# Three groups' transposes and copies ahead of their distance products, and the context norms added on VectorE, in a one-core gated cross-attention kernel

## The chip, the cores and the metric

The kernel runs on one core of a Trainium2 chip. The metric is the device time of one execution in microseconds (us), lower is better. Engines: TensorE multiplies matrices into PSUM, ScalarE (ACT in the profile) evaluates activations, VectorE (DVE) does elementwise work, GpSimd (POOL) does some of both, and SyncE (SP) issues most transfers. Each engine runs its own instructions in order; semaphores join them.

## What is computed

Inputs are `x` and a context, 32 samples of 128 rows by 128 features. Four parts follow each other, each added to `x`: gated attention of `x` on the context, a quantized feed-forward layer, an alignment of each sample's rows with its context rows, and eight experts behind a global threshold. The change touches the seam between the second and the third:

```python
# second part, its last product
acc = jnp.einsum('bsh,oh->bso', xq - zx, wq)
return acc * (sx * sw) + b
...
# third part: a = context of one sample, b = layernorm(x) of that sample
def _pairwise_euclidean(a, b):
    aa = jnp.sum(a * a, axis=-1)[:, None]
    bb = jnp.sum(b * b, axis=-1)[None, :]
    ab = a @ b.T
    return jnp.sqrt(jnp.maximum(aa + bb - 2.0 * ab, 0.0))
...
D = _pairwise_euclidean(small, large)
R = _dtw_cost(D)          # R[i,j] = D[i,j] + min of three neighbours
```

The table R is walked back to an alignment, which picks the context rows that are added to `x`.

## The kernel before

**Tiles.** Samples go in groups of 4 (`GB`)[...]. The alignment is split in two parts: the first 12 samples (`NP = 3` groups) and the other 20. The first part's distances are made in the stage that the change touches. The second part's are made by ScalarE, TensorE and GpSimd (`second_dense`, L1226) while VectorE runs the first part's alignment.

**The stage.** `dense_steps` (L950) loops over the three groups. For each, `dense` (L903) quantizes the hidden layer (VectorE L906, ScalarE L909, VectorE L910), multiplies it by the second weight (TensorE L916) and adds to `X` (VectorE L921). `norm_steps` (L193), fed in between, makes the layer norm of groups 0 and 1 together and then of group 2: statistics (L155 on), a root by Newton steps (L182 to L190), the normalized rows `y` (VectorE L211) and their transposes into the PSUM tile `tp` (TensorE L215). Then it calls `take`, which calls `distances` (L924) for the group:

- ScalarE copies `tp` twice: `ym2` is minus two times it (L926), `ysq` its square (L928).
- TensorE sums in `d2`: `ones` times `ysq` (L931) puts the square norms of `y` in every row, and four products of the context `CD` with `ym2` (L933) add the cross terms.
- ScalarE adds the context norms `aa`, one number per row and sample, and clips at zero (`dd`, L939, once for each of four samples).
- ScalarE takes roots, rows 0 to 63 forward (L941) and rows 64 to 127 with the columns reversed (L942), into `dist`. The last of these is kept as `held["root"]`.
- Two transfers a group put the halves of `dist` into the DRAM tensor `d_dram` (L945), on SP's queue, except that the last group's second half goes on ScalarE's.

The pool `dist` holds two buffers of each of `hqt`, `ym2`, `ysq`, `dd` and `dist`; `distps` holds two PSUM banks each of `tp` and `d2`.

**Behind it.** `warp_steps` (L969) loads chunks of `d_dram` into `dc` (L1056, on SP) and runs the alignment rows on VectorE: two instructions a row, a minimum (L1072) and a scan (L1073), 64 rows. Then tables and a walk back (`hit`, L1101). `second_dense` starts on ScalarE behind `held["root"]` (L1162). The expert stage begins with `aligned(0)` (L1301) and holds 64 units of matmuls (L1470, L1483), between which VectorE's background steps (`pump`, L1408) do the second part's alignment and the threshold search (L1352).

**Order.** The code order isn't the order on the engines. A planner takes the whole program with its dependences and arranges each engine's instructions by the costs that it assumes; `tc.issue_after` adds an edge. Before, TensorE runs the transposes of groups 0 and 1, products 0 and 1, the transposes of group 2, product 2.

Of the kernel before, what the change touches and what calls it, by code (L numbers as in the profile page):

```python
# [8 lines left out]
F32 = mybir.dt.float32  # L9
# [3 lines left out]
AF = mybir.ActivationFunctionType  # L13
ALU = mybir.AluOpType
# [4 lines left out]
P = 128  # L19
B = 32  # L20
S = 128
# [7 lines left out]
GB = 4  # L29
# [4 lines left out]
SH = S // 2  # L34
# [3 lines left out]
NP = 3  # L38
# [5 lines left out]
def tile_flamingo_gated(  # L44
# [21 lines left out]
    nc = tc.nc  # L66

    def pool(stack, name, bufs=1, space=None, side=None):
        kw = {} if space is None else {"space": space}
        kw.update({} if side is None else {"side": side})  # L70
        return stack.enter_context(tc.tile_pool(name=name, bufs=bufs, **kw))

    def new(p, shape, dt, tag, bufs=None):
        kw = {} if bufs is None else {"bufs": bufs}
        return p.tile(shape, dt, tag=tag, name=tag, **kw)
# [7 lines left out]
    CD = new(keep, [P, B, S], F32, "CD")  # L83
# [45 lines left out]
    ones = new(keep, [P, P], F32, "ones")  # L129
# [18 lines left out]
    held = {}  # L148
# [44 lines left out]
    def norm_steps(p, psp, s0, n, take, tag, shape=None):  # L193

        xq = X[:, s0 : s0 + n, :]
        m, w = (8, "") if n <= 8 else (16, "_w")
        mean = new(p, [P, m], F32, "bn_mean" + w)[:, 0:n]
        r = new(p, [P, m], F32, "bn_r" + w)[:, 0:n]
        for _ in row_norm_steps(p, xq, n, mean, r):
            yield  # L200
        for h in range(n // GB):
            if shape is None:
                tp = new(psp, [P, GB, S], F32, tag)
            else:
                if h % 2 == 0:
                    pair = new(psp, shape, F32, tag)
                tp = pair[:, h % 2]
            for i in range(GB):
                j = GB * h + i
                y = new(p, [P, D], F32, "y", bufs=6)  # L210
                got = nc.vector.tensor_scalar(  # L211
                    y, xq[:, j, :], mean[:, j : j + 1], r[:, j : j + 1], ALU.subtract, ALU.mult
                )
                held["y"] = getattr(got, "ins", got)
                nc.tensor.transpose(tp[:, i, :], y, ident)  # L215
                if i % 2 == 1:
                    yield
            take(s0 // GB + h, tp)
            yield
# [70 lines left out]
    with ExitStack() as st:  # L290
# [47 lines left out]
        for k in range(2):  # L338
            nc.gpsimd.affine_select(
                out=mtmp[:, k], in_=mtmp[:, k], compare_op=ALU.is_ge, fill=0.0, base=-64 * k,  # L340
# [3 lines left out]
                out=mtmp[:, k], in_=mtmp[:, k], compare_op=ALU.is_ge, fill=0.0,  # L344
# [7 lines left out]
        for k in range(2):  # L352
            nc.gpsimd.affine_select(
                out=mneg[:, k], in_=mneg[:, k], compare_op=ALU.is_ge, fill=-BIG, base=SH - SH * k,
# [44 lines left out]
        for k in range(6):  # L399
# [3 lines left out]
                rhs=one_c[0:1, :], start=True, stop=True,  # L403
# [6 lines left out]
        for k in range(2):  # L410
            hr_ps = new(p_at, [P, 4, S], F32, "at")
            nc.tensor.matmul(
                hr_ps, lhsT=sel.rearrange("p j c h -> p (j c h)"),
                rhs=ind[:, 4 * k : 4 * k + 4, :], start=True, stop=True,
# [89 lines left out]
        def take(g, tp):  # L504
            nc.scalar.copy(YT[:, GB * g : GB * g + GB, :], tp)
            v = YT[:, GB * g : GB * g + GB, :].rearrange("p b s -> p (b s)")
            nc.vector.tensor_reduce(xst[:, 0, g : g + 1], v, AX.X, ALU.max)
            nc.vector.tensor_reduce(xst[:, 1, g : g + 1], v, AX.X, ALU.min, negate=True)
# [137 lines left out]
        def finish(s0, n, HN, d2, ms):  # L646
# [30 lines left out]
            for _ in norm_steps(lp, p_at, s0, n, take, "at"):  # L677
                yield
# [39 lines left out]
        for p in range(B // 2 + 1):  # L718
# [4 lines left out]
            for u in range(3):  # L723
# [6 lines left out]
                g = p // 2 + 1  # L730
# [47 lines left out]
    for n_s in (BP, B - BP):  # L778
        m = new(rest, [2 * n_s, 3], F32, f"mask{len(masks)}")
        for v, fill, low_side in ((0, -1.0, True), (1, -2.0 * S - 2.0, True), (2, 1.0, False)):  # L780
            nc.gpsimd.memset(m[:, v : v + 1], fill)
            nc.gpsimd.affine_select(
                out=m[:, v : v + 1], in_=m[:, v : v + 1], compare_op=ALU.is_ge, fill=0.0,
# [7 lines left out]
    d_dram = new(dram, [2, B, SH, S], F32, "d_dram")  # L791
# [6 lines left out]
    with ExitStack() as st:  # L798
# [18 lines left out]
        with ExitStack() as st2:  # L817
# [16 lines left out]
            def rounded(n):  # L834
                for k in range(2):
                    blk = YT[:, 8 * n + 4 * k : 8 * n + 4 * k + 4, :].rearrange("p b s -> p (b s)")
                    nc.scalar.activation(blk, blk, AF.Identity, bias=magic_c, scale=inv)
                    xq = XQ[:, 1024 * n + 512 * k : 1024 * n + 512 * k + 512]
                    nc.scalar.activation(xq, blk, AF.Relu, bias=low_x[:, 1:2])
                    got = nc.vector.tensor_scalar(xq, xq, 255.0, low_x[:, 0:1], ALU.min, ALU.add)  # L840
                return getattr(got, "ins", got)

            rounded(0)
            for n in range(4):
                for c in range(NC):
                    ph = new(p_h, [P, 2, 512], F32, "ph")
                    for k in range(2):
# [3 lines left out]
                            start=True, stop=True,  # L851
# [8 lines left out]
                    if c == 0 and n < 3:  # L860
                        got = rounded(n + 1)
# [15 lines left out]
        aa = new(rest, [P, B], F32, "aa")  # L877
# [43 lines left out]
        nc.vector.scalar_tensor_tensor(xb, po, s2, xb, ALU.mult, ALU.add)  # L921
        yield 0.7

    def distances(g, tp, dp, d2_new, queues):  # L924
        ym2 = new(dp, [P, GB, S], F32, "ym2")
        nc.scalar.activation(ym2, tp, AF.Copy, scale=-2.0)  # L926
        ysq = new(dp, [P, GB, S], F32, "ysq")
        nc.scalar.activation(ysq, tp, AF.Square)  # L928
        d2 = d2_new()
        dd = new(dp, [P, GB, S], F32, "dd")  # L930
        nc.tensor.matmul(d2, lhsT=ones, rhs=ysq, start=True, stop=False)  # L931
        for i in range(GB):
            nc.tensor.matmul(  # L933
                d2[:, i, :], lhsT=CD[:, GB * g + i, :], rhs=ym2[:, i, :],
                start=False, stop=(i == GB - 1),
            )
        for i in range(GB):
            b = GB * g + i
            nc.scalar.activation(dd[:, i, :], d2[:, i, :], AF.Relu, bias=aa[:, b : b + 1])  # L939
        dist = new(dp, [P, GB, S], F32, "dist")  # L940
        nc.scalar.activation(dist[0:SH], dd[0:SH], AF.Sqrt)  # L941
        got = nc.scalar.activation(dist[SH:P], dd[SH:P, :, ::-1], AF.Sqrt)  # L942
        held["root"] = getattr(got, "ins", got)
        for h in range(2):
            queues[h].dma_start(  # L945
                out=d_dram[h, GB * g : GB * g + GB].rearrange("b r j -> r b j"),
                in_=dist[SH * h : SH * h + SH],
            )

    def dense_steps(tie, dp, lp, po_new, psp, tag, take):  # L950
        ties = [tie, tie]
        behind = iter(())
        for n in range(NP):
            for _ in dense(n, ties[n], dp, po_new, ties):
                for _ in range(3):
                    next(behind, 0)
            if n % 2 == 1 or n == NP - 1:
                for _ in behind:
                    pass
                m = n % 2 + 1  # L960
                behind = norm_steps(lp, psp, GB * (n - m + 1), m * GB, take, tag)
        for _ in behind:
            pass
# [166 lines left out]
    with ExitStack() as st:  # L1130
        dp = pool(st, "dist", bufs=2)
        lp = pool(st, "lnA", bufs=2)
        p_o = pool(st, "p_o", bufs=2, space=PSUM)
        dps = pool(st, "distps", bufs=2, space=PSUM)

        def take(g, tp):
            distances(
                g, tp, dp, lambda: new(dps, [P, GB, S], F32, "d2"),
                (nc.sync, nc.scalar if g == NP - 1 else nc.sync),
            )  # L1140

        dense_steps(
            held["quantized"], dp, lp, lambda: new(p_o, [P, GB, D], F32, "po"), dps, "tp", take
        )
    parts[0].close()

    with ExitStack() as st:
        wp = pool(st, "warp", bufs=2, side="right")  # L1150
        w1p = pool(st, "warp1", side="right")
        dp = pool(st, "distB", side="right")
# [3 lines left out]
        dps = pool(st, "distpsB", space=PSUM)  # L1156
# [128 lines left out]
    with ExitStack() as st:  # L1285
# [176 lines left out]
        for n, (k, p, g, j) in enumerate(units):  # L1462
# [5 lines left out]
            for c in range(NC):  # L1468
                ph = new(p_h, [P, GB * S], F32, "mph")
                got = nc.tensor.matmul(  # L1470
                    ph, lhsT=w1e[:, j, c * P : (c + 1) * P], rhs=tok, start=True, stop=True
                )
                held["mm"] = getattr(got, "ins", got)
                hT.append(new(hp, [P, GB * S], F32, "hT"))
                got = nc.scalar.activation(  # L1475
                    hT[c], ph, AF.Gelu_apprx_tanh, bias=mb1s[:, e, c : c + 1]
                )
# [3 lines left out]
            for i in range(GB):  # L1481
                for c in range(NC):
                    got = nc.tensor.matmul(  # L1483
                        po[:, i, :], lhsT=hT[c][:, i * S : (i + 1) * S], rhs=w2e[:, j, c, :],
                        start=(c == 0), stop=(c == NC - 1),
                    )
# [55 lines left out]
```

## Time and profile before

| what | value |
|---|---|
| time, median of 3 runs | 868.48 us (868.47 to 871.42) |
| profiled execution | 869.44 us, span 867.7 us |
| TensorE busy | 692.2 us (80%), mean granted clock 0.861 |
| VectorE busy | 588.4 us (68%) |
| ScalarE busy | 453.2 us (52%) |
| `ym2`, L926, 128x512 from PSUM | 3 times, mean 605 ns |
| `ysq`, L928, 128x512 from PSUM | 3 times, mean 598 ns |
| `dd`, L939, 128x128 from PSUM | 12 times, mean 368 ns; four in a row 1.14 us |
| `dist`, L941 and L942, 64x512 | 3 times each, mean 629 and 626 ns |
| table load before the first root | once, 1283 ns |
| `d_dram<-dist`, L945 | 6 transfers, 128 KB each |

Granted clock in the windows of the stage, from the profile: 0.50 from 242 to 246 us, 0.60 from 246 to 248, 1.00 from 248 to 254, 0.60 from 254 to 256, 0.50 from 256 to 268.

How to read it: the profile shows one execution, on the time axis of its span. A product of 128x512 in f32 appears as two instructions, one of 128x128 also as two, so "L933 x8" is one group's four products. The chain of waits is followed back from the last instruction to what released it, and lists its pieces in order of time: start, length, engine, tile and line. In a timeline a row ends with the idle time before it in brackets and with what released it.

### The profile page before, as it was taken

To read this page: it belongs to the slowest core of one execution; us is meant where nothing else is said; L and a number is where in the kernel's file an instruction comes from. 1 tells how busy PE (TensorE), PEld (TensorE's weight loads), DVE (VectorE), ACT (ScalarE), POOL (GpSimd) and SP (SyncE) were. 2 spreads that over 40 slices of the span, in tenths; PEclk is the share of its full clock that TensorE was granted. 3 is DMA by queue.
4 is the path that set the end of the run, shared out by engine and by line. 5 is a ranking of instruction groups with operands and counts; after the bars stand their busy time and mean duration, and the time that the engine had idled before them with its cause. 6 is when DMAs were issued, how large, how long until landed. Compare 5 with 4: busy or idle time off the path is not lost.

```text
span 867.7 us, 13245 instructions
## 1 busy us (share of the span) xinstructions
PE 692.2 (80%) x4689; PEld 462.3 (53%) x4695; DVE 588.4 (68%) x2040; ACT 453.2 (52%) x803; POOL 66.8 (8%) x132
## 2 busy tenths in 40 slices
PE   5798998344251334478999999999999999999997
PEld 2244554211231222246777776876677777777775
DVE  7847998979835998879995376656614544444444
ACT  2778777496248978433444444434444333334442
POOL 2000000001301121100100101010000000000000
PEclk9898999555565555559999999999999999999999
DMA  8100000200012131012452111020013212121110
GB/s 322 37 2 12 2 3 2 81 18 0 0 25 52 29 73 44 13 35 80 145 158 89 62 62 61 25 74 37 37 39 96 62 37 85 37 61 49 50 61 25
DMA packets 20201, 47.32 MB, mean 55 GB/s; under 512 B 4014, under 2 KB 6942, under 8 KB 20110
## 3 DMA queue, kind: packets, MB, share of 16 engines
q1 hardware_dynamic: 14372, 29.69, 11.1%
q0 software_dynamic: 5056, 16.62, 6.1%
q8 instruction: 37, 0.61, 0.3%
q10 hardware_dynamic: 706, 0.16, 0.1%
q14 instruction: 30, 0.25, 0.1%
HBM read 27.12 MB, written 13.37 MB: 47 GB/s over the span
## 4 chain that ended last, share of the span: by engine, by line
PE 54%; DVE 20%; ACT 2%; issue 2%; DMA 1%; POOL 0%; SPq 0%; DVEq 0%; ACTq 0%
PE mph L1470 25%; PE mpo L1483 24%; DVE ru L1073 4%; DVE ru L1072 3%; DVE hit L1101 3%; DVE hst L858 2%; DVE hst L859 2%; PE px L1313 1%; PE small L1333 1%; DVE junk L1347 1%; PE po L916 1%; PE px L1327 1%; PE d L931 0%; DVE bn L155 0%; DVE lf L993 0%
## 5 line engine op out<-in xcount | busy, mean ns | idle before, releaser
L1483 PEld LDWEIGHTS mpo<-mw,hT 128*128 128x128 f32 x2048 | 249.6, 192 | 58.9 <-issue 39.4
L1475 ACT ACTIVATE hT<-mph,mb1s 128x512 f32<-128x512 f32 x256 | 175.7, 687 | 182.0 <-PE mph L1470 168.4
L1483 PE MATMUL mpo<-mw,hT 128*128 128x128 f32 x2048 | 256.1, 276 | 0.1
L1470 PE MATMUL mph<-YT,mw 128*128 128x512 f32 x512 | 245.3, 600 | 0.0
L1470 PEld LDWEIGHTS mph<-YT,mw 128*128 128x128 f32 x512 | 87.4, 193 | 57.9 <-issue 57.8
L1433 DVE TENSOR_TENSOR biased<-mpo,mb2s 128x512 f32<-128x512 f32 x28 | 19.4, 691 | 119.6 <-PE mpo L1483 119.6
L1438 DVE SCALAR_TENSOR_TENSOR X<-biased,GA,X 128x128 f32<-128x128 f32 x248 | 67.8, 345 | 0.1
L1491 ACT COPY ye<-mpo 128x512 f32<-128x512 f32 x34 | 19.9, 585 | 86.2 <-PE mpo L1483 83.6
L1073 DVE TENSOR_TENSOR_SCAN ru<-ru,dc 24x128 f32<-24x128 f32 (+1 forms) x128 | 54.0, 422 | 6.8 <-DMA dc<-d_dram 3.3
L1072 DVE TENSOR_TENSOR ru<-ru 24x128 f32<-24x128 f32 (+1 forms) x128 | 38.8, 303 | 3.1
L1492 POOL DMA_DIRECT2D y_dram<-ye x34 | 18.5, 543 | 228.4 <-ACT ye L1491 228.0
L562 ACT ACTIVATE dm<-bi 128x512 f32<-128x512 f32 x48 | 29.0, 606 | 8.0 <-PE bi L557 3.2
L604 DVE TENSOR_TENSOR sm<-sc,dm 128x512 f32<-128x512 f32 x32 | 21.7, 684 | 13.9 <-ACT dm L562 9.8
L1194 PE MATMUL po<-w2q,HT 128*128 128x128 bf16 x80 | 9.4, 313 | 24.6 <-ACT HT L1167 24.6
L849 PE MATMUL ph<-XQ,w1q 128*128 128x512 bf16 x31 | 15.6, 615 | 16.8 <-DVE XQ L840 9.5
L1261 PE MATMUL tp<-ident,y 128*128 128x128 f32 x20 | 8.1, 475 | 23.9 <-ACT y L1167 23.9
L1203 PE MATMUL d<-b,ones 128*128 128x512 f32 x10 | 10.0, 1107 | 18.0 <-ACT b L1167 18.0
L1101 DVE SCALAR_TENSOR_TENSOR hit<-jotab,vw,YT 24x128 bf16<-24x128 bf16 x59 | 21.1, 357 | 4.1 <-DMA YT<-dv 2.0
L518 ACT ACTIVATE qm<-YT,mcol 128x512 f32<-128x512 f32 x32 | 23.2, 732 | 0.0
L1433 DVE TENSOR_TENSOR biased<-yl,mb2s 128x512 f32<-128x512 f32 x34 | 23.1, 681 | 0.0
L538 PE MATMUL sc<-qm,CD 64*128 64x256 f32 x128 | 21.7, 449 | 0.6 <-ACT YT L379 0.6
L1194 PEld LDWEIGHTS <-HT 128*128 128x128 bf16 x80 | 8.1, 147 | 26.1 <-ACT HT L1167 26.1
(380 smaller groups left out, 1019.5 us busy)
## 6 DMA issues: line engine op xcount, KB each, us to landing
y_dram<-ye POOLq DMA_DIRECT2D x34, 256.0 KB, 2.3
yl<-y_dram SPq DMA_DIRECT2D x34, 256.0 KB
mw<-in_mw POOLq DMA_DIRECT2D x12, 512.0 KB, 4.5
rblk<-ru SPq DMA_DIRECT2D x10, 288.8 KB
X<-in_x SPq DMA_DIRECT2D x4, 512.0 KB
CD<-in_ctx_d SPq DMA_DIRECT2D x4, 512.0 KB
CT<-in_ctx_t SPq DMA_DIRECT2D x4, 512.0 KB
mw<-in_mw SPq DMA_DIRECT2D x4, 512.0 KB
```

What stands on the lines that cost most here:

```text
L518: nc.scalar.activation(held["qm", g][:, h], YT[:, GB * g : GB * g + GB, :], AF.Copy, scale=mcol[:, h : h + 1],)
L538: nc.tensor.matmul(scs[:, k, 4 * v : 4 * v + 4], lhsT=CD[kr, n, :], rhs=qm[kr, :, n % GB, SH:S], start=True, stop=True,)
L562: done = nc.scalar.activation(dm, bi, AF.Exp)
L604: got = nc.vector.tensor_tensor(sm, scs[:, u], dm, ALU.mult)
L1072: nc.vector.tensor_tensor(u, ru[:, r, 0, 1 : S + 1], ru[:, r, 0, 0:S], ALU.min)
L1073: got = nc.vector.tensor_tensor_scan(ru[:, r + 1, 0, 1 : S + 1], u, dc[:, r, :], BIG, ALU.min, ALU.add)
L1101: nc.vector.scalar_tensor_tensor(hit, jotab[0:H2], vw[:, r + 1 : r + 2], near[:, r - r0, :] if r >= r0 else DV[:, r, :], ALU.is_le, ALU.mu ...
L1433: nc.vector.tensor_tensor(t, y, bias, ALU.add)
L1438: nc.vector.scalar_tensor_tensor(X[:, b, :], v[:, i, :], GA[:, E * b + e : E * b + e + 1], X[:, b, :], ALU.mult, ALU.add,)
L1470: got = nc.tensor.matmul(ph, lhsT=w1e[:, j, c * P : (c + 1) * P], rhs=tok, start=True, stop=True)
L1475: got = nc.scalar.activation(hT[c], ph, AF.Gelu_apprx_tanh, bias=mb1s[:, e, c : c + 1])
L1483: got = nc.tensor.matmul(po[:, i, :], lhsT=hT[c][:, i * S : (i + 1) * S], rhs=w2e[:, j, c, :], start=(c == 0), stop=(c == NC - 1),)
```

## The change

`distances` goes. `take` now makes only the two copies `ym2` and `ysq` of a group, each in three buffers instead of two, and keeps them in a list. After `dense_steps` has written out all three groups, a loop over the list makes the products, the sum with the context norms, the roots and the transfers. The sum with `aa` and the clip at zero are one VectorE instruction for each sample in place of one ScalarE instruction. The roots, the buffers of `dd` and `dist`, the queues of the transfers and `held["root"]` stay as they were.

```diff
-    def distances(g, tp, dp, d2_new, queues):
-        ym2 = new(dp, [P, GB, S], F32, "ym2")
-        nc.scalar.activation(ym2, tp, AF.Copy, scale=-2.0)
-        ysq = new(dp, [P, GB, S], F32, "ysq")
-        nc.scalar.activation(ysq, tp, AF.Square)
-        d2 = d2_new()
-        dd = new(dp, [P, GB, S], F32, "dd")
...
-        for i in range(GB):
-            b = GB * g + i
-            nc.scalar.activation(dd[:, i, :], d2[:, i, :], AF.Relu, bias=aa[:, b : b + 1])
...
+        normed = []
+
         def take(g, tp):
-            distances(
-                g, tp, dp, lambda: new(dps, [P, GB, S], F32, "d2"),
-                (nc.sync, nc.scalar if g == NP - 1 else nc.sync),
-            )
+            ym2 = new(dp, [P, GB, S], F32, "ym2", bufs=NP)
+            nc.scalar.activation(ym2, tp, AF.Copy, scale=-2.0)
+            ysq = new(dp, [P, GB, S], F32, "ysq", bufs=NP)
+            nc.scalar.activation(ysq, tp, AF.Square)
+            normed.append((g, ym2, ysq))
...
+        for g, ym2, ysq in normed:
+            d2 = new(dps, [P, GB, S], F32, "d2")
+            nc.tensor.matmul(d2, lhsT=ones, rhs=ysq, start=True, stop=False)
+            for i in range(GB):
+                nc.tensor.matmul(
+                    d2[:, i, :], lhsT=CD[:, GB * g + i, :], rhs=ym2[:, i, :],
+                    start=False, stop=(i == GB - 1),
+                )
+            dd = new(dp, [P, GB, S], F32, "dd")
+            for i in range(GB):
+                b = GB * g + i
+                nc.vector.tensor_scalar(
+                    dd[:, i, :], d2[:, i, :], aa[:, b : b + 1], 0.0, ALU.add, ALU.max
+                )
+            dist = new(dp, [P, GB, S], F32, "dist")
+            nc.scalar.activation(dist[0:SH], dd[0:SH], AF.Sqrt)
+            got = nc.scalar.activation(dist[SH:P], dd[SH:P, :, ::-1], AF.Sqrt)
+            held["root"] = getattr(got, "ins", got)
+            for h in range(2):
+                (nc.sync, nc.scalar if g == NP - 1 else nc.sync)[h].dma_start(
+                    out=d_dram[h, GB * g : GB * g + GB].rearrange("b r j -> r b j"),
+                    in_=dist[SH * h : SH * h + SH],
+                )
```

More of the change, by code (lines that the diff above doesn't have):

```diff
@@ L922, in dense @@
         yield 0.7
-    def distances(g, tp, dp, d2_new, queues):
-        ym2 = new(dp, [P, GB, S], F32, "ym2")
-        nc.scalar.activation(ym2, tp, AF.Copy, scale=-2.0)
-        ysq = new(dp, [P, GB, S], F32, "ysq")
-        nc.scalar.activation(ysq, tp, AF.Square)
-        d2 = d2_new()
-        dd = new(dp, [P, GB, S], F32, "dd")
-        nc.tensor.matmul(d2, lhsT=ones, rhs=ysq, start=True, stop=False)
-        for i in range(GB):
-            nc.tensor.matmul(
-                d2[:, i, :], lhsT=CD[:, GB * g + i, :], rhs=ym2[:, i, :],
-                start=False, stop=(i == GB - 1),
-            )
-        for i in range(GB):
-            b = GB * g + i
[L939 to L948, printed above, removed]
     def dense_steps(tie, dp, lp, po_new, psp, tag, take):
@@ L1134, in tile_flamingo_gated @@
         dps = pool(st, "distps", bufs=2, space=PSUM)
+        normed = []
         def take(g, tp):
-            distances(
-                g, tp, dp, lambda: new(dps, [P, GB, S], F32, "d2"),
-                (nc.sync, nc.scalar if g == NP - 1 else nc.sync),
-            )
+            ym2 = new(dp, [P, GB, S], F32, "ym2", bufs=NP)
[3 more added lines that the diff above has]
+            normed.append((g, ym2, ysq))
         dense_steps(
```

## The prediction

> **What bounds the kernel now.** I read the page's slices first: TensorE is at 9 tenths from slice 18 on (the expert stage, a fixed amount of matmul), and before that its clock stands at 5 with gaps in its row, so there something else decides. Then the chain of waits over 222 to 275 us of the profiled execution, where the edited stage lies. It runs through that stage without a break and out of it over a DMA into the alignment rows on VectorE:
>
> ```profile
> 244.13 0.60 ACT ym L926
> 244.73 0.50 ACT ysq L928
> ...
> 245.27 2.07 PE d L931 x2
> 247.34 1.08 PE d L933 x8
> ...
> 248.45 1.14 ACT dd L939 x4
> ...
> 249.61 1.28 ACT L941
> 250.90 0.63 ACT dist L941
> ...
> 252.21 1.14 ACT dd L939 x4
> 253.35 0.49 ACT ym L926
> 253.83 0.49 ACT dist L941
> ...
> 254.35 0.63 ACT dist L942
> ...
> 255.00 0.60 ACT ysq L928
> ...
> 255.65 2.08 PE d L931 x2
> 257.72 1.72 PE d L933 x8
> ...
> 261.29 2.44 DMA d_dram<-dist
> ```
>
> The second column is how long each piece holds the chain. ScalarE serves three groups in a row; the copies of the third (ym at 253.35, ysq at 255.00) come behind the roots of the first two, so the third product starts only at 255.65. From the last root's end (261.29 + 0.63 = 261.92) to the first scan (268.10) it is 6.18 us of DMA out, issue, and DMA in. TensorE's own timeline shows what the late copies cost it:
>
> ```profile
> 248.25 1.02 PE L931 MATMUL d<-ysq,ones 128*128 128x512 f32 x2
> 249.11 1.05 PE L933 MATMUL d<-ym,CD 128*128 128x128 f32 x8
> 250.00 0.60 PE L215 MATMUL tp<-ident,y 128*128 128x128 f32 x4
> 255.65 2.08 PE L931 MATMUL d<-ysq,ones 128*128 128x512 f32 x2 [5.05 <-ACT ysq L928]
> ```
>
> The second product takes 1.9 us (248.25 to 250.16) at granted clock 1.00; the third, after 5.05 us of idling, 3.8 us (255.65 to 259.44) at 0.50. Everything after the first scan hangs on it: rows and hits on VectorE to 367, the first expert matmul at 381.7, then TensorE busy for 476 of the 484 us from 384 to 868 (24.6, 111.2, 107.1 and 233.1 in four windows). ScalarE's second stage starts at 261.94 from the same root. So I carry a shift of the last root one for one to the end.
>
> **The change, step by step**, on the clock of the profiled execution.
>
> *Transposes and copies.* Up to 245.27 nothing differs: the transposes of groups 0 and 1 and their copies already run ahead of product 0. The third group's y tiles leave VectorE at 247.21 (246.09 + 1.12). The planner seems to give an idle engine the ready instruction that stands first in the code (before, ym2 slipped in front of dist 1, whose operand was just not ready), so I let it start product 0 at 245.27 and put the third transposes next, now ahead of product 1: product 0 ends at 248.42, transposes at 249.02 (0.60), copies at 249.07 + 0.60 + 0.50 = 250.17. No root stands before them any more.
>
> *Products.* Product 1 from 249.02 ends at 251.0, product 2 follows at once, 1.9 us warm: 252.95. That is 6.5 us before today's 259.44, 1.9 of it from the clock.
>
> *Norms on VectorE.* Twelve ScalarE instructions go (three times 1.14 us) and twelve VectorE ones come. No row shows a two-operation tensor_scalar from PSUM at 128x128 f32. The nearest are y L211, same operation from SBUF, 341 ns, and X<-mpo L1438, same size from PSUM, 344 ns, 0.273 apart where 248 of its SBUF form follow each other. By them four cost 3 x 0.273 + 0.344 = 1.16 us. The Trainium skill speaks against the move ("VectorE: DVE Perf Modes", section on why PSUM operands drop a tier): f32 from PSUM loses the double rate that a scalar operation has from SBUF. At 0.96 GHz that is 67 ns on 128 elements, 408 each, 1.4 us for four; below 1.1 nothing speaks. I take 1.16, as the L1438 row reads PSUM. dd of group 0 ends 249.61, of group 2 at 254.15 (254.4 by the rule). VectorE has nothing else here: its next instruction before was at 264.63. What queues behind a dd on it are only those four memsets of the alignment.
>
> *Roots.* The table load (1.28) waited for its activation's operand elsewhere (at 383.82, right after the first expert product), so it starts behind both the copies and dd 0: 250.2 to 251.5. Roots 0 end at 252.78, roots 1 at 254.1 (0.63 each plus 0.03).
>
> *The new wait.* dist has two buffers, and group 2 writes the one of group 0, whose two transfers are issued at 252.1 and 252.8. One took 2.44 us to land, the ScalarE-issued one some 2.65 (the alignment's first memset, freed by it, ran at 264.63). Before, group 2 came 8 us later and never met this. Now buffer 0 is free at about 255.3, 1.2 us after dd 2 and roots 1. Bounds: nothing (6.4 us gained in all), or a wait for the first half alone (root end 256.0), or both halves; the copy b in the second stage waits 2.4 us for d_dram<-b with both halves out, so I take both: roots 2 run 255.35 to 256.64. Behind this wait on ScalarE stands only its second stage, tied to the last root anyway. It also covers the norms: dd 2 could be 1 us later for nothing.
>
> *DMAs.* The same six. The five on SP take 0.58 to 0.70 us to issue and their sources come every 0.66, so SP keeps step. ScalarE's one stays last. The first two moved 262 KB inside 251.6 to about 255; pairs may overlap a little more, 0 to 0.5 us. Two more copies of ym2 and ysq are 4 KB per partition and no time.
>
> *Sum*: 261.92 - 256.64 = 5.3 us. The profiled execution took 869.44 (span 867.7 and 1.74 around it), 0.96 over the median of the runs; the difference is taken from the median: **868.48 - 5.3 = 863.2**.
>
> **The clock as a rule.** The row shows the clock rising near 247.3, 4.5 us after the first transpose. The skill ("TensorE: Matmul & The Clock Gate", Part 1) says the window of some 3.4 us runs freely and the start of full speed varies from run to run. By the row the gain is 5.3; by the rule's latest phase (two windows, 249.6) product 0 and the third transposes stay cold: copies end 251.4, roots 0 at 254.0, buffer free at 256.5, last root 257.9, gain 4.0. Two of three runs agree to 0.01 us, so I take the row.
>
> **Rivals.**
>
> *The plan leaves the third transposes behind product 1* (the change doesn't do all it says). For: they stood there before. Against: in the code they now come first. They end at 250.6, dd 0 is ready at 249.6, so table load and a root pass before ym2; ysq2 ends at about 252.7, product 2 at 254.9 warm or 256.5 cold, dd 2 at 256.0 to 257.7, last root 257.4 to 259.0: gain 2.9 to 4.5, **864.8**.
>
> *Cold clock*, as above: **864.5**.
>
> *The gain is taken back later*, a transfer or ScalarE's second stage ending last: **868**. Against: last copies at 361.6 wait on a TensorE queue held by the alignment (9.06 us before a<-d), so ScalarE has slack.
>
> *Slower: the plan of the search is redrawn.* All engines' orders come from one plan. At 580 to 629 us, 31 rounds each put one TensorE product (L1349) that waits for a VectorE count between expert matmuls; today TensorE waits 0.2 us there in all. The count and its three neighbours hold VectorE about 1 us per round and rounds stand from 1.4 us up. Were fewer matmuls put between, TensorE would wait up to 0.5 us a round, 15 in all. It outweighs the gain from 0.17 us a round (5.3 / 31); at 0.35 the time is 868.5 - 5.3 + 10.9 = **874**. Against: nothing there changes, and both sides shift alike.
>
> **How the numbers follow.** Forecast 0.62 (range 862.1 to 864.2), late transposes 0.14, cold 0.06, taken back 0.06, slower plan 0.12. Half a per cent, about what this kernel's measurement can tell from none, is 4.34 us. Faster: 0.60 of the forecast, 0.04, 0.02: 0.66. Within: 0.02, 0.10, 0.04, 0.06 and 0.02 of the slower plan: 0.24. Slower: 0.10. The range goes from 861.8 (no buffer wait, a little more) to 867.0, which takes in late transposes and cold clock and leaves the last two cases out.
>
> **What would show it.** Right: third copies before any root; product 2 about 1.9 us with no gap ahead; dd on VectorE near 0.34 us; an idle of about 1 us on ScalarE before group 2's root that ends on d_dram<-dist; first scan near 262.8; the expert stage as long as before. Wrong: copies behind a root; dd 2 far over 1.4 us; a wait put ahead of dd on VectorE; or a first scan near 262.8 with the end not moved.

## The result, and the profile after

| | before | after |
|---|---|---|
| median time of 15 runs each | 868.48 us (866.38 to 872.59) | 861.8 us (859.47 to 868.63) |
| span of the profiled execution | 867.7 us | 861.2 us |
| last root of the stage ends, behind the start of the first copy `ym2` | 17.79 us | 11.55 us |
| first scan of the alignment, behind the same point | 23.97 us | 17.58 us |
| from the first scan to the end | 599.60 us | 599.41 us |

The ratio is 0.991, with a 95% interval of 0.989 to 0.9931: 6.0 to 9.6 us faster. The ratio itself stands for 7.8 us; the medians differ by 6.7 us, the profiled spans by 6.5. The forecast was 5.3 us, 863.2: the direction was right and the gain too small, by about one microsecond in the traces and in the medians, and by more in the ratio, for which the traces give no reason. In the trace that microsecond lies within the edited stage: its last root comes 6.24 us earlier, measured from the first copy, and what follows the first scan is as long as before.

TensorE's timeline of the changed kernel (start, length, engine, line, operation; the idle time before a row stands in brackets):

```profile
242.87 2.27 PE L215 MATMUL tp<-ident,y 128*128 128x128 f32 x8 [3.71 <-DVE y L211]
245.35 2.07 PE L1125 MATMUL d<-ysq,ones 128*128 128x512 f32 x2 [0.21 <-ACT ysq L1116]
247.21 0.76 PE L215 MATMUL tp<-ident,y 128*128 128x128 f32 x4
247.81 1.06 PE L1127 MATMUL d<-ym,CD 128*128 128x128 f32 x8
248.70 1.02 PE L1125 MATMUL d<-ysq,ones 128*128 128x512 f32 x2
249.56 1.05 PE L1127 MATMUL d<-ym,CD 128*128 128x128 f32 x8
250.45 1.02 PE L1125 MATMUL d<-ysq,ones 128*128 128x512 f32 x2
251.31 1.05 PE L1127 MATMUL d<-ym,CD 128*128 128x128 f32 x8
```

The gap of 5.05 us is gone, and product 2 takes 1.9 us (250.45 to 252.36). The third transposes do not stand behind product 0, where the forecast put them, but inside it: behind its 512-column part and ahead of its four small products. ScalarE's timeline over the same stage:

```profile
248.01 0.60 ACT L1114 ACTIVATE ym<-tp 128x512 f32<-128x512 f32 x1 [1.74 <-PE tp L215]
248.50 0.59 ACT L1116 ACTIVATE ysq<-tp 128x512 f32<-128x512 f32 x1
249.11 1.28 ACT L1138 ACT_TABLE_LOAD   x1
250.41 0.63 ACT L1138 ACTIVATE dist<-dd 64x512 f32<-64x512 f32 x1
251.06 0.63 ACT L1139 ACTIVATE dist<-dd 64x512 f32<-64x512 f32 x1
251.82 0.63 ACT L1138 ACTIVATE dist<-dd 64x512 f32<-64x512 f32 x1
252.47 0.63 ACT L1139 ACTIVATE dist<-dd 64x512 f32<-64x512 f32 x1
254.48 0.63 ACT L1138 ACTIVATE dist<-dd 64x512 f32<-64x512 f32 x1 [1.38 <-DMA d_dram<-dist]
255.13 0.63 ACT L1139 ACTIVATE dist<-dd 64x512 f32<-64x512 f32 x1
```

And `dd` of group 0 on VectorE:

```profile
248.90 1.13 DVE L1134 TENSOR_SCALAR dd<-d,aa 128x128 f32<-128x128 f32 x4 [0.18 <-PE d L1127]
```

Two things are to be seen together. The third copies are done at 249.09, and the table load starts at 249.11, while the norms of group 0, whose result the root behind it reads, end only at 250.03. So the load did not wait for the root's operand; it runs beside the norms, and the root starts as soon as the table is there. The third thing is the wait of 1.38 us before the roots of group 2: `dist` has two buffers, and the chain of waits shows that wait as the path of the stage:

```profile
251.82 0.03 ACT dist L1138
251.84 2.53 DMA d_dram<-dist
...
254.48 0.64 ACT dist L1138
...
255.14 2.45 DMA d_dram<-dist
...
257.67 0.33 SPq L1030
258.05 0.35 SPq L1030
258.44 0.36 SPq L1030
258.92 2.77 DMA dc<-d_dram
...
261.79 0.42 DVE ru L1047
```

The transfer that ends the wait runs from 251.84 to 254.37 and carries the second half of group 0's roots, which end at 251.69. So both halves had to be out, as the forecast took it. SP issues three loads (`SPq`) ahead of the one that the first scan waits for; that matters further on.

### The profile page after: what moved, and what is told of

It reads as the page before. It is cut to its first block, busy times and chain, and to the rows that moved or that the text cites. A ratio compares the mean times of both kernels' runs of the same rounds, so it can differ in the third digit from the quotient of the medians.

```text
span 861.2 us, 13247 instructions
## 1 busy us (share of the span) xinstructions
PE 692.2 (80%) x4689; PEld 462.1 (54%) x4695; DVE 592.2 (69%) x2052; ACT 450.1 (52%) x791; POOL 66.3 (8%) x132
## 4 chain that ended last, share of the span: by engine, by line
PE 54%; DVE 20%; issue 2%; DMA 1%; ACT 1%; POOL 0%; SPq 0%; DVEq 0%; ACTq 0%
PE mph L1471 25%; PE mpo L1484 24%; DVE ru L1047 4%; DVE ru L1046 3%; DVE hit L1075 3%; DVE hst L858 2%; DVE hst L859 2%; PE px L1314 1%; PE small L1334 1%; DVE junk L1348 1%; PE po L916 1%; PE px L1328 1%; DMA d_dram<-dist 1%; PE d L1125 0%; DVE bn L155 0%
```

## The experiments

The stages ahead of the edit vary from execution to execution, so a position is told in microseconds behind the start of the first copy `ym2` in the same trace. Row 13 is the first scan of the second chunk of 12 rows, told behind the first scan.

| run | first copy at | last root ends | first scan | row 13 | first scan to end | first copy to end |
|---|---|---|---|---|---|---|
| before | 244.13 | 17.79 | 23.97 | 10.47 | 599.60 | 623.57 |
| changed | 244.21 | 11.55 | 17.58 | 10.41 | 599.41 | 616.99 |
| e1 norms only | 241.45 | 15.48 | 21.68 | 10.44 | 598.97 | 620.65 |
| e2 norms on ScalarE | 250.00 | 13.12 | 19.42 | 10.34 | 598.28 | 617.70 |
| e3 load behind norms | 240.74 | 12.78 | 18.83 | 10.40 | 599.03 | 617.86 |
| e4 transposes behind product 0 | 244.75 | 12.75 | 18.91 | 10.47 | 599.24 | 618.15 |
| e5 three buffers | 250.01 | 10.55 | 15.46 | 13.41 | 600.93 | 616.39 |
| e6 load early | 244.07 | 11.12 | 17.10 | 10.43 | 599.53 | 616.63 |
| e7 e5 and e6 | 249.90 | 10.56 | 15.27 | 13.44 | 601.33 | 616.60 |
| e8 e7, memset moved | 242.76 | 10.58 | 15.33 | 13.49 | 601.31 | 616.64 |
| e9 loads in order | 241.31 | 11.76 | 16.14 | 13.49 | 599.15 | 615.29 |
| e10 changed again | 250.24 | 11.36 | 17.40 | 10.43 | 599.36 | 616.76 |
| e11 six loads, three buffers | 241.13 | 10.90 | 15.78 | 10.37 | 597.89 | 613.67 |
| e12 six loads | 242.48 | 11.85 | 16.24 | 10.43 | 597.98 | 614.22 |

The two traces of the changed kernel (changed and e10) differ by 0.19 in the last root and 0.23 from the first copy to the end. e9 and e12 leave the code up to the last root as it is in the changed kernel, and over these four traces the last root spreads from 11.36 to 11.85, so a difference below 0.5 us says little by itself. Part of this scatter goes with the moment at which TensorE's granted clock passes from 0.50 to 1.00. A quarter of a microsecond of e10 and of e12 in which that happens (columns: window, length, busy time and instructions of TensorE, weight loads, VectorE, ScalarE and GpSimd, then TensorE's granted clock):

```profile
252.99:253.24 0.25, 0.25 (x2) 0.02 (x1) 0.12 (x1) 0.00 (x0) 0.00 (x0) 0.61 0.00 0
```

```profile
246.23:246.48 0.25, 0.25 (x3) 0.25 (x2) 0.00 (x0) 0.00 (x0) 0.00 (x0) 0.53 0.00 0
```

Counted from the start of the first transposes (248.90 and 241.14), the clock rises after 4.3 us in e10 and after 5.3 in e12; worked out in the same way it is 4.7 in the changed trace and 5.1 in e9. The third copies end 4.70, 5.19, 4.88 and 5.10 behind the first copy, in the same order. So a row is best compared with one of these four whose clock rises at a like moment: e2 and e5 (4.3 and 4.4) with e10, e6 (4.7) with changed, e3 and e11 (5.0 and 5.1) with e9, e4 (5.3) with e12. Single runs of e3, e4, e5 and e6 took 860.28, 864.66, 868.09 and 862.39 us; they follow the place of the first copy more than the edit, so these four are judged by the columns behind it.

### One half of the change alone: e1 and e2

e1 keeps the old order and moves only the norms:

```diff
-            nc.scalar.activation(dd[:, i, :], d2[:, i, :], AF.Relu, bias=aa[:, b : b + 1])
+            nc.vector.tensor_scalar(
+                dd[:, i, :], d2[:, i, :], aa[:, b : b + 1], 0.0, ALU.add, ALU.max
+            )
```

> The kernel before with only the norms moved to VectorE; order of transposes and products as before. On the axis of the kernel before (last root ends 261.92). Theory, the order is what pays and the norms alone bring less than half: roots 0 start at the end of dd 0, near 249.6, the copies of group 3 still come behind roots 1 and end near 253.7, product 3 starts there after some 3 us of idling; last root between 258.2 (product warm, 1.9 us) and 260.1 (cold, 3.8 us): 1.8 to 3.7 us earlier than before. Rival, the freed ScalarE is the whole gain: last root near 255.8, as in the changed kernel, 6 us earlier. If the table load waits for dd 0 as I had assumed, it starts near 249.6 and not right behind the fourth copy (near 246.2), and the gain is only about 1 us.

Median 864.42 us, ratio 0.9957 (0.9942 to 0.9972). The first scan comes 2.29 us earlier than before. TensorE's timeline of e1 still shows the late third product, half of it at the slow clock:

```profile
250.95 1.68 PE L931 MATMUL d<-ysq,ones 128*128 128x512 f32 x2 [3.20 <-ACT ysq L928]
252.42 1.92 PE L933 MATMUL d<-ym,CD 128*128 128x128 f32 x8
```

and on its ScalarE the load again runs ahead of its operand, here by more than 3 us:

```profile
243.53 1.28 ACT L943 ACT_TABLE_LOAD   x1
246.76 0.63 ACT L943 ACTIVATE dist<-dd 64x512 f32<-64x512 f32 x1 [1.95 <-DVE dd L939]
```

e2 is the opposite half, the changed kernel with the norms back on ScalarE:

```diff
-                nc.vector.tensor_scalar(
-                    dd[:, i, :], d2[:, i, :], aa[:, b : b + 1], 0.0, ALU.add, ALU.max
-                )
+                nc.scalar.activation(dd[:, i, :], d2[:, i, :], AF.Relu, bias=aa[:, b : b + 1])
```

> The changed kernel with the norms back on ScalarE; copies first, as changed. Changed kernel: last root ends 255.76. Theory: from the end of the sixth copy (249.1) ScalarE has 3 x 1.14 of norms, 1.28 of table load and 6 x 0.65 of roots in one row, so the last root ends near 257.8, 2.0 us later than in the changed kernel and 4.1 earlier than before; the wait for the buffer disappears, being covered. Rival, the norms were hidden anyway: last root within 0.4 us of 255.76.

Median 862.23 us, ratio 0.9933 (0.991 to 0.9957). The first scan comes 4.55 us earlier than before: the order is the larger half. 2.29 and 4.55 make 6.84, against 6.39 for both, so the halves nearly add. With the order in place, the norms bring another 1.84 (19.42 to 17.58). The last root of e2 comes 1.57 later than in the changed trace and 1.76 later than in e10, where 2.0 was expected. In e2 the norms of the three groups hold ScalarE's path for 1.04, 1.29 and 0.94 us, 3.3 together; 1.38 of it comes back in the changed kernel as the buffer wait, which e2 does not have.

### Where the missing microsecond was: e3 and e4

The forecast had the third copies end at 250.17 and the load start at 250.2; they ended at 249.09 and it started at 249.11. Two things differ, where the transposes stand and what the load waits for. e3 makes the load wait for the norms, with one small copy that reads `dd`, tied ahead of the first root, and keeps the order:

```diff
+            if g == 0:
+                tiny = new(dp, [P, 1], F32, "tiny", bufs=1)
+                got = nc.scalar.activation(tiny, dd[:, GB - 1, 0:1], AF.Copy)
+                held["tiny"] = getattr(got, "ins", got)
-            nc.scalar.activation(dist[0:SH], dd[0:SH], AF.Sqrt)
+            with tc.issue_after(held["tiny"]):
+                nc.scalar.activation(dist[0:SH], dd[0:SH], AF.Sqrt)
```

> The changed kernel with one ScalarE copy of a single column of dd 0 ahead of the first root, so that the table load stands behind the end of dd 0. Theory (the term that I mis-sized is the table load, which I let wait for dd 0): load from about 250.3 to 251.6 instead of 249.1 to 250.4, roots 0 end near 252.9, the buffer comes free near 255.6, last root ends near 256.9: 1.2 us later than in the changed kernel, first scan near 262.9, close to the forecast's 262.8. Rival (the load is not on the path, the missing microsecond lies elsewhere): later by no more than the copy itself, 0.3 us.

ScalarE of e3:

```profile
246.77 0.20 ACT L1139 ACTIVATE tiny<-dd 128x1 f32<-128x1 f32 x1 [0.97 <-DVE dd L1134]
246.97 1.28 ACT L1143 ACT_TABLE_LOAD   x1
248.27 0.63 ACT L1143 ACTIVATE dist<-dd 64x512 f32<-64x512 f32 x1
```

The load now stands behind the norms, and the last root comes 1.23 us later than in the changed trace, 1.02 later than in e9, whose clock rises at a like moment. The small copy's own 0.20 us is in this, so the free load is worth 0.8 to 1.0 us.

e4 leaves the load alone and puts the third transposes where the forecast had them, behind all of product 0, by writing product 0 in the code ahead of the third group's norm:

```diff
+            if g == 0:
+                held["d2"] = product(g, ym2, ysq)
...
-            d2 = new(dps, [P, GB, S], F32, "d2")
...
+            d2 = held["d2"] if g == 0 else product(g, ym2, ysq)
```

> The changed kernel with product 0 written out ahead of the third group's norm, so that the third transposes run behind the whole of product 0, the order that the forecast assumed (in the changed kernel they run inside it). Theory: transposes end near 249.1, copies near 250.2 instead of 249.1, table load to 251.5, last root near 256.8: 1.1 us later than in the changed kernel, the forecast's sum. dd 0 ends 0.4 us earlier, which brings nothing, because copies and load end last. Rival (place inside product 0 doesn't matter): last root within 0.3 us of 255.76.

TensorE of e4:

```profile
247.75 1.53 PE L1116 MATMUL d<-ym,CD 128*128 128x128 f32 x8
249.12 0.60 PE L215 MATMUL tp<-ident,y 128*128 128x128 f32 x4
```

The last root comes 1.20 us later than in the changed trace, 0.90 later than in e12. Either one alone costs about as much as the 0.96 that the forecast missed by, because the load is held by the later of two things: the third copies, which stand ahead of it on ScalarE, and its own wait, if it has one. The last root of e4 stands 12.75 behind the first copy; the forecast's stood at 256.64 - 244.13 = 12.51. With the forecast's order the kernel does what the forecast said, to 0.24 us, which is within the scatter.

### The new wait: e5, e6, e7

e5 gives `dist` a third buffer:

```diff
-            dist = new(dp, [P, GB, S], F32, "dist")
+            dist = new(dp, [P, GB, S], F32, "dist", bufs=NP)
```

> The changed kernel with three buffers of dist, so that group 2 does not wait for the transfers of group 0. Theory (the buffer is the last wait of the stage, then comes dd 2, which ends at 253.60): the 1.38 us of idling on ScalarE goes, roots 2 start at 253.6 and end at 254.9, 0.86 us earlier, first scan near 260.9. Rival (the transfers, now closer together, collide): last root 0.86 earlier, but the last pair takes over 3.2 us to land instead of 2.45, and the scan moves by less than 0.3 us.

The wait is gone (0.53 us for `dd` is left in its place) and the last root comes 1.00 earlier, 0.81 against e10; 0.86 was expected. The first scan moved by more, 2.12, and by the end 1.5 of it was lost again: row 13 stands 13.41 behind the first scan instead of 10.41. VectorE of e5, at the seam of the first two chunks:

```profile
278.11 0.14 DVE L1036 MEMSET ru<- 24x104 f32 x1 [2.31 <-DMA rblk<-ru]
```

The planner had moved that memset, which prepares the third chunk, ahead of row 13, and it waits for the transfers of the row blocks. I took it for the cause.

e6 brings the table load forward, with a one-column root behind the last `hq` of `dense` (L909):

```diff
-        nc.scalar.activation(hq, blk, AF.Relu, bias=low[:, 1:2])
+        relu = nc.scalar.activation(hq, blk, AF.Relu, bias=low[:, 1:2])
+        if n == NP - 1:
+            pre = new(dp, [P, 1], F32, "pre", bufs=1)
+            with tc.issue_after(getattr(relu, "ins", relu)):
+                nc.scalar.activation(pre, one_c, AF.Sqrt)
```

> The changed kernel with a one-column root behind the third quantization, so that the table load lies in ScalarE's idle time before the transposes. Theory: roots 0 start at the end of dd 0 (250.05 instead of 250.41), the whole tail moves by 0.36 us, last root at 255.4. Rival (the copies or the wait for the buffer hold it): no change within 0.1 us. A second load of the table anywhere would undo it.

Last root 0.43 earlier, scan 0.48, with 0.93 us of the buffer wait left. The expected 0.36 fits, but this is one trace and no more than the scatter; either way a load that is hidden for the most part is worth little. e7 joins e5 and e6:

> Three buffers of dist and the early table load together. Theory: dd 2 (end 253.6) holds the last roots in both cases, so it gives what three buffers give alone, last root at 254.9, 0.86 us earlier than the changed kernel; time about 0.9 below the changed kernel's, which five rounds may not tell apart. Rival (the two add up): 1.2 us earlier.

It does not add up: 10.56 and 15.27, hardly other than e5 alone, and row 13 late again. Median 863.51 us, ratio 0.9921 (0.9886 to 0.9955), no better than the change as it is.

### Who takes it back: e8 to e12

e8 is e7 with that memset, and the one that belongs to it, tied behind row 8 of the chunk before (`held["row"]` is the scan of that row):

```diff
-            nc.vector.memset(ru[:, :, :, S : S + 4], 0.0)
+            tied = s0 == 0 and r0 >= 24
+            with tc.issue_after(held["row"]) if tied else ExitStack():
+                nc.vector.memset(ru[:, :, :, S : S + 4], 0.0)
...
```

> The kernel of e7 (third buffer for the roots, table load early), in which the memset of the scan's start values is put behind row 8 of the chunk before, so that it no longer stands ahead of the scan's rows in VectorE's queue. Theory (e5 and e7 lost their gain because that memset waits for the row blocks' transfers while rows are queued behind it): the first scan stays 15.3 us after the first copy, as in e7, and the stretch behind it comes back from 601.3 to 599.4; from the first copy to the end 614.7, 2.3 below the changed kernel's 616.99. Rival (the scan has caught up with something else that was hidden behind the late start, such as the loads of the chunks to come): the stretch behind the first scan stays above 600.5, and from the first copy to the end it is 616 or more.

My theory fell. The memset is out of the way, yet row 13 stands at 13.49 and nothing is gained. VectorE of e8 names another releaser for that row:

```profile
271.58 0.41 DVE L1056 TENSOR_TENSOR_SCAN ru<-ru,dc 24x128 f32<-24x128 f32 x1 [3.15 <-DMA dc<-d_dram]
```

and SP's queue tells why (x is the number of transfers in a row):

```profile
255.89 1.95 SPq L1034 DMA_DIRECT2D dc<-d_dram  x5
260.06 8.49 SPq L1072 DMA_DIRECT2D rblk<-ru  x4
268.59 1.35 SPq L1034 DMA_DIRECT2D dc<-d_dram  x3
```

The first two chunks are loaded in six transfers. Before and in the changed kernel all six go out first, but in an order in which the fourth is the one that the first scan waits for (the chain above). With the third buffer the planner orders them better for the first scan, which in e5's chain waits for the second, and puts the sixth, the second chunk's other half, behind the four transfers of row blocks, which wait for scanned rows. Row 13 needs it, and gets it 3 us late. e9 changes only the order of the loads, with two buffers:

```diff
+                    with tc.issue_after(held["load"]) if s0 == 0 and "load" in held else ExitStack():
+                        got = queue.dma_start(
...
+                    held["load"] = getattr(got, "ins", got)
```

> The changed kernel with SP's loads of the distances held to the written order (first half, second half, chunk by chunk), buffers and table load as they are. Theory (in e5 one of the 2.1 us came from the order of SP's loads and not from the buffer): last root 11.5 after the first copy, as in the changed kernel, and the first scan 4.9 instead of 6.0 behind the last root, so 16.5 after the first copy against 17.58. If the hoisted memset follows from this order and not from the buffer, the stretch behind the first scan is 600.5 to 601.5, and nothing is gained in the end. Rival (the loads' order follows from the buffer and is worth nothing alone): first scan at 17.4 to 17.7, and 599.4 behind it.

The first scan comes 16.14 behind the first copy, 1.44 earlier than in the changed kernel: a good order of loads is worth that without any buffer. Row 13 is late by 3 us as in e5, which was expected to cost the gain; but the end moved by 1.7 (615.29), so that part of the expectation missed. With the same late row e5 has 600.93 behind its first scan and e9 599.15; half of the difference lies before `ge` (the step looked at below) and half behind it, and its cause stays open. One run of e9, 858.3 us.

e10 is the changed kernel once more, next to e8 and e9 on one chip:

> The changed kernel once more, beside e8 on the same chip. Both theories: last root 11.5, first scan 17.6 after the first copy, 599.4 behind it, 617.0 from the first copy to the end, wherever the first copy falls (240 to 250); ratio to the kernel before 0.992.

Median 862.02 us, ratio 0.9933 (0.99 to 0.9966); e8 beside it 862.11 us, 0.994 (0.9911 to 0.9968).

e11 and e12 put all six loads in the written order ahead of the row blocks, e11 with three buffers, e12 with two:

```diff
+            for k0, m0 in CHUNKS[0:2] if s0 == 0 and r0 == 0 else ((r0, n),):
+                if k0 in loaded:
+                    continue
+                loaded[k0] = new(wp, [H2, rows, S], F32, "dc")[:, 0:m0, :]
...
+                        with tc.issue_after(held["load"]) if s0 == 0 and "load" in held else ExitStack():
```

> The changed kernel with three buffers for the roots, and with all six loads of the first two chunks on SP in the written order and ahead of the first chunk's row blocks. In e8 and e9 the sixth load (the second chunk's second half) stood behind the four transfers of row blocks, which wait for the scan's rows, and the second chunk's first row waited for it. Theory (that load, and not the memset, took the gain back): last root 10.6 and first scan 15.3 to 15.5 after the first copy; the 13th scan 10.4 behind the first, as in the changed kernel, instead of 13.4 to 13.5; 599.4 from the first scan to the end, so 614.7 to 614.9 from the first copy on, 2.1 to 2.3 below the changed kernel. Rival (an engine beside the scan sets the end of the first part's scan stage, so that an earlier start is not carried): the 13th scan comes as in the changed kernel, and 600.5 or more remain behind the first.

> The same six loads in order, with two buffers as in the changed kernel. Theory: last root 11.5, first scan 16.4 after the first copy, the 13th 10.4 behind it, 599.4 to the end: 615.8 from the first copy on, 1.2 below the changed kernel; the buffer is worth the 1.0 between this and e11. Rival: 616.5 or more.

SP's queue in e12:

```profile
256.22 2.68 SPq L1035 DMA_DIRECT2D dc<-d_dram  x6
260.75 8.48 SPq L1069 DMA_DIRECT2D rblk<-ru  x4
269.33 0.89 SPq L1035 DMA_DIRECT2D dc<-d_dram  x2
```

Row 13 is back at 10.37 and 10.43 with the early first scan kept: the sixth load was the cause of the late row. e11 has a median of 857.86 us, ratio 0.9878 (0.9852 to 0.9903), e12 857.66 us, 0.9871 (0.9848 to 0.9894). From the first copy to the end both are faster than the change as it was made, by 2.5 to 3.3 us. Their medians lie about 4 us below its median, but they were not timed beside it, and the intervals of the ratios (0.989 to 0.9931 for the change) overlap a little. The third buffer, worth 0.95 at the last root (0.86 against e9), leaves 0.46 at the first scan and 0.55 at the end, which the times do not show.

The order of the loads accounts for 1.34 us of e12's gain, at the first scan. Both kernels also end 1.4 to 1.5 us better behind the first scan than expected. The chain of waits of the changed kernel shows where most of that comes from, at the end of the first alignment:

```profile
360.93 0.73 PE d L1206 x2
361.65 0.55 PE ends_ps L1095 x2
362.20 0.72 PE d L1206 x2
362.93 0.56 PE ends_ps L1095 x2
363.51 0.19 DVE ends L1098
...
363.83 0.29 DVE ge L1311
```

Two pairs of the second part's distance products (`d` L1206, 1.45 us) run between the last products of the walk. In e12 the chain goes another way through the same seam:

```profile
355.97 1.29 PE d L1214 x6
...
358.52 0.64 ACT b L1176
...
359.25 0.48 DVE ge L1319 x2
```

and TensorE and VectorE of e12 read:

```profile
357.28 0.30 PE L1092 MATMUL vt<-ident,vw 24*64 24x24 f32 x2
```

```profile
358.93 0.18 DVE L1106 COPY ends<-ends_ps 128x24 f32<-128x24 f32 x1 [0.99 <-PE ends_ps L1103]
```

The distance products end at 357.26, before the walk's own products begin, and nothing stands between those any more: from the last row of `hit` to `ge` it is 2.10 us instead of 3.33, 1.2 of the 1.4 to 1.5. The chain names ScalarE's root `b` (to 359.16) as what released `ge`, but `ge` starts 0.32 us behind the start of `ends`, which it reads, in the changed kernel as here, so the root was only just in time. e5, e8 and e9 have 1.62 in that place. There the granted clock was 1.00 (e5, 367 to 369 us), in e12 0.50 (357 to 359). This also names the likely next limit: in e12 the walk follows the second part's last distance product by 0.02 us, so a still earlier first part would find TensorE taken. That is argued from the trace and was not tried.

## Why the prediction was right, and where it was wrong

- *The chain, and a shift carried one for one to the end*: right. 599.41 us remain behind the first scan, 599.60 before. The rival of a gain taken back later did not come for this change; it came, in another place than named, when e5 moved the scan further.
- *Third copies ahead of every root, product 2 at 1.9 us without a gap*: right, and e1 shows the price without it.
- *Norms on VectorE*: 1.13 us for four, 345 ns each in the mean; 1.16 was forecast from the row with a PSUM source. The prediction's estimate from the Trainium skill ("VectorE: DVE Perf Modes", section on why PSUM operands drop a tier) would have made 408 ns each. At 128 elements the lost double rate did not show (345 ns from PSUM here, 341 from SBUF in the y row before), and the measurement decides; whether the row from SBUF has that rate at this size, no run here shows. VectorE was not as empty as forecast: the planner put six memsets (248.05 to 248.72) ahead of dd 0 and the alignment's first minimum (249.94) behind it, which cost the path nothing.
- *The failed step*: "copies at 249.07 + 0.60 + 0.50 = 250.17", and "it starts behind both the copies and dd 0: 250.2 to 251.5". The term is the start of the table load: 249.11, not 250.2. The third transposes were put as a whole behind product 0, while the planner orders single instructions: the third y tiles leave VectorE at 247.09, and the transposes start at 247.21, ahead of product 0's four small products. Why the planner took them first is not on record. And the load was given its activation's operand as a wait, from one row at 383.82. e3 and e4 each take away one of the two and bring the last root to within 0.3 us of the forecast. Had only one of them been seen, the forecast would hardly have changed.
- *The new wait*: right in kind, 1.38 us against the 1.25 forecast (254.1 to 255.35). It gives back part of the earlier load: roots 0 end 1.09 us earlier than forecast, the last root 0.88 on the clock of each profile.
- *The sum*: 12.51 forecast behind the first copy, 11.55 measured. This 0.96 us is the larger part of the 1.4 between the forecast's 5.3 and the medians' 6.7. Between the last root and the first scan another 0.15 is gained, and 0.19 behind it, both within what two traces of one kernel differ by.
- *The clock*: the row was the right choice for this stage. The start of full speed does vary from execution to execution, as the prediction quotes: over all traces it lies 4.3 to 5.3 us behind the first transposes, against the 4.5 that the row was read for. The 6.8 of the latest phase came in none. The reason given, "Two of three runs agree to 0.01 us", was a weak one: over 15 runs the kernel before spreads from 866.38 to 872.59.
- *The other rivals*: late transposes, and a slower plan of the search, did not come.

## What to carry to other kernels

When a step sits on the path, ask of each instruction, not of each group, where an in-order engine will put it, and take "it waits for its operand" only from a row of the same kind at the same place. A gain at one point is kept only if the next queue is as ready as its first consumer: after moving a stage, look at the order of the transfers behind it, which here was worth more (1.34 us at the first scan) than the buffer wait that the profile pointed at. And compare runs from a point just ahead of the edit, not from the start.

## What the runs showed of the hardware

The table load ran ahead of the semaphore that its activation waited for, in the changed kernel by 0.92 us (249.11 against the end of the norms at 250.03), and in e1 by more than 3. Before the expert stage the load goes on starting right behind the first expert product (383.82 before, 377.44 after, both behind an idle of 3.91 us on the `mph` product); what makes that one late was not tried.

Executions of one and the same kernel differ in the clock that the early stages are granted, and in time with it. The window from 80 to 120 us of the changed kernel, and then of its repetition in e10 (columns as above):

```profile
80.00:120.00 40.00, 37.03 (x572) 20.23 (x566) 37.21 (x119) 32.75 (x73) 0.00 (x0) 0.96 0.01 2
```

```profile
80.00:120.00 40.00, 38.49 (x507) 20.67 (x506) 31.60 (x104) 29.53 (x64) 0.00 (x0) 0.80 0.01 2
```

At 0.96 the first copy starts at 244.21, at 0.80 at 250.24, and the spans are 861.2 and 867.0; from the first copy on they agree to 0.23 us. Over all traces the first copy stood at 240.7 to 242.5 where that window had 1.00, at 244.1 to 244.8 for 0.95 and 0.96, and at 249.9 to 250.2 for 0.80 (e8, with 0.91, at 242.8, is out of this order). Whether the clock alone moves the first copy was not tried, but the first copy stands ahead of the edited stage, and in single traces it lay up to 9.5 us apart (240.7 to 250.2).
